# Four chained layers on one core: pools that wait by tile, a reordered norm, the second Sobel layer's first two pairs prepared inside the first's drain, and last pairs in halves

## The chip, the core and the metric

One program runs on one core of a Trainium2 chip. The core has a matrix engine (PE, with its weight loads as PEld), a vector engine (DVE), an activation engine (ACT), a general engine (POOL) and a queue that starts most transfers (SP). They run side by side and wait for each other by semaphores. The metric is the device time of one execution in microseconds (us), as the median of several runs; lower is better.

## The reference, cut to what matters

The input x is an image of 256 rows, 256 columns and 32 channels, in 32-bit floats. Each layer adds to x a function of its group norm (16 groups of two channels over the whole image).

```
x = x + attention(_gn(x))     # softmax over an axis of length 1, so: sigmoid(mn @ Wg) * (mn @ Wv) @ Wo + bo
                              # with mn the layer norm of _gn(x) over the 32 channels
x = x + sobel(_gn(x))         # pooled = 3x3 average; sqrt(grad_x**2 + grad_y**2 + 1e-6), both 3x3 Sobel, per channel
x = x + sobel(_gn(x))
x = x + recurrent(_gn(x))     # two gated cells with a group norm in each, 256 steps along the columns of the image
```

A group norm needs the mean and the variance of the whole image, so no layer can finish its norm before the one ahead has written all of its output.

## The kernel before, in words

**Layout.** The image stays in on-chip memory as `xa` (and `xb`): 128 partitions are four neighbouring columns times 32 channels, the free axis is 64 blocks of four columns by 256 rows. Two blocks are a *pair*, 512 values per partition; all stages work pair by pair, 32 in all (`NST`). Statistics of a pair are taken by `bn_stats` on DVE as soon as the pair is written, and combined by one `bn_aggr`; a matmul with `K_GN` then sums over the partitions of a channel group (first the mean `pm`, then, from `q`, the variance `pv`).

**Input and first norm** (to 35 us). Twenty loads, transposes on PE (L243), copies on ACT (L250), statistics on DVE (L251); `busy_here` puts matmuls on junk behind the first two input groups. Then `bn_aggr` (L267), five `busy_ln` fillers (L272), the mean (L276), the variance (L284), eight records of small bias matmuls (L288), the comparison of the cell's norm weights, and the products of the two weight matrices with the centring (L300). ACT copies the biases (L317) and scales the two products into `wv4` and `wg4` (L319). `shifted(k)` subtracts the mean from a pair, on DVE (L308) but for pair 2 on ACT (L303).

**Layer norm** (35 to 62 us). For each of eight groups of four pairs PE centres (L366), ACT squares (L390), PE averages (L347). After the first group's variance ACT takes the deviation (`std`, L357), DVE the reciprocal `rstds[0]` (L380), and SP issues four broadcast DMAs per pair (`rows`, L328). `scaled(k)` multiplies a pair by its rows: DVE for pair 0, POOL for all others (L338). The deviation of group 0 stands in ACT's order behind the first square of group 2.

**Attention** (58 to 288 us). A list of work with due times, `plan`, is repeated every `step` and sorted; its order is that of the instructions. Matmuls for values and gates (L459), sigmoid on ACT (L468), product on DVE (L472), output matmuls (L485), bias on ACT (L500), residual on POOL (L501), statistics on DVE (L504).

**Sobel layers** (288 to 411 and 411 to 537 us), both by `sobel_layer`. `shift` does the norm's mean and variance, with fillers (`busy`, L580): 3 ahead, 2 between, 16 behind. The mean enters through `m15` and `m75` (L586, L587). Per pair: `convert` (ACT, L601) subtracts 1.5 means; `twos` and `threes` (DVE, L605, L620) sum neighbours along the rows into `pp`, with `ends` (ACT, L610) for the first and last row; `difference` (POOL, L636) makes `dh`; `fours` and `smooth` (L628, L632) make `v` and `sh`, on DVE for pairs 0 and 1 and on POOL for the others. `mixed` (PE, L670) does the step across columns in PSUM, with neighbouring pairs as input. Then `square` (ACT, L676), twice, `total` (DVE, L680), `root` (ACT, L684), `residual` (DVE, L687) and `statistics` (DVE, L690). The second square, the total's second input and the root are one PSUM tile. The order of instructions is again that of a list sorted by due times, one pair each `every` = 3.6; behind the last `mixed` stand seven fillers (L733). The tile pools are opened and closed in each layer.

**Recurrence** (546 to 2490 us): the second layer's output goes to DRAM and back as `xt`, and 256 steps follow.

Of the kernel before, what the change touches and what calls it, by code (L numbers as in the profile page):

```python
# [18 lines left out]
S = 256  # L19
# [4 lines left out]
P = 128  # L24
# [37 lines left out]
def net_kernel(  # L62
# [54 lines left out]
    wv4 = big2.tile([P, D], F32, name="wv4")  # L117
    wg4 = big2.tile([P, D], F32, name="wg4")
# [22 lines left out]
    def new_stats():  # L141
        return small.tile([P, NST, nc.vector.BN_STATS_DIM], F32, name="stats")
# [49 lines left out]
    with tc.tile_pool(name="nat", bufs=6, side="right") as natp, tc.tile_pool(  # L192
# [37 lines left out]
        warm = ps_in.tile([P, P], F32, name="warm", bufs=1)  # L230

        def busy_here(n):
            for _ in range(n):
                nc.tensor.matmul(warm, lhsT=ident, rhs=ident, start=True, stop=True)

        busy_here(7)
        for i, (nat, w0, wl) in enumerate(nats):
            for b2 in range(wl // (2 * J)):
                pt = ps_in.tile([P, 2, 2, P], F32, name="pt")
                for b in range(2):  # L240
                    for h in range(2):
                        lo = (b2 * 2 + b) * J
                        nc.tensor.transpose(  # L243
                            pt[:, b, h, :],
                            nat[:, h, lo : lo + J, :].rearrange("p w c -> p (w c)"),
                            ident,
                        )
                blk = w0 // J + b2 * 2
                dst = xa[:, blk : blk + 2, :].rearrange("p b s -> p (b s)")
                nc.scalar.copy(dst, pt.rearrange("p b h s -> p (b h s)"))  # L250
                nc.vector.bn_stats(stats[:, blk // 2, :], dst)  # L251
            if i < 2:
                busy_here(3)
        table(AF.Sqrt, xa[:, NB - 1, 0:1])

    big3 = second.enter_context(tc.tile_pool(name="big3", bufs=1, side="right"))
# [4 lines left out]
    ps_at = psums.enter_context(tc.tile_pool(name="ps_at", bufs=1, space=PSUM))  # L261
# [12 lines left out]
    busy_ln(5)  # L274
    pm = bank(1)[:, 0:1]
    nc.tensor.matmul(pm, lhsT=kg[:, K_GN, :], rhs=mv[:, 0:1], start=True, stop=True)  # L276
    less = small.tile([P, 1], F32, name="less")
# [7 lines left out]
    pbias = bank(3)  # L285
    for i, w in enumerate(wone):
        for half in range(2):
            nc.tensor.matmul(  # L288
                pbias[:, 2 * i + half : 2 * i + half + 1],
                lhsT=w[:, half * P : (half + 1) * P],  # L290
                rhs=beta,
                start=True,
                stop=True,
            )
    compare()
    psame = bank(6)[0:1, 0:1]
    total_same(psame)
    pws = [bank(4 + i)[:, 0:D] for i in range(2)]
    for pw, w in zip(pws, wgam):
        nc.tensor.matmul(  # L300
            pw, lhsT=cen4.rearrange("c j k -> c (j k)"), rhs=w, start=True, stop=True
        )
    nc.scalar.activation(pair(xb, 2), pair(xa, 2), AF.Identity, bias=less)  # L303
    gstd = small.tile([P, 1], F32, name="gstd")
    nc.scalar.activation(gstd, pv, AF.Sqrt, bias=gn_eps)

    def shifted(k):
        nc.vector.tensor_scalar(pair(xb, k), pair(xa, k), one, less, ALU.mult, ALU.add)  # L308

# [6 lines left out]
    decide(psame, flag)  # L316
    nc.scalar.copy(wbias, pbias[:, 0:4].rearrange("p (i h) -> p i h", i=2))  # L317
    for w, pw in zip((wv4, wg4), pws):
        nc.scalar.activation(w, pw, AF.Copy, scale=scale)  # L319
# [20 lines left out]
    with tc.tile_pool(name="lnq", bufs=9) as lnq:  # L340
# [20 lines left out]
        for g in range(GROUPS):  # L361
# [15 lines left out]
            for j, pc in enumerate(pcs):  # L377
                if g == EARLY + 1 and j == 1:
                    std = deviations()
                    nc.vector.reciprocal(rstds[0], std)  # L380
                    for k in range(3):
                        rowsets[k] = rows_of(k)
                    for k in range(5 * J, NST):
                        shifted(k)
                    for f in reduces:
                        f()
                    for k in range(3):
                        scaled(k)
                sqs.append(lnq.tile([P, 2 * S], F32, name="sq"))
                nc.scalar.activation(sqs[-1], pc, AF.Square)  # L390
# [49 lines left out]
    with tc.tile_pool(name="at", bufs=3) as atp:  # L440
# [13 lines left out]
        def one_of(o, u, j, k):  # L454
            bias = lambda i: wbias[:, i, u : u + 1]
            if o in ("v", "g"):
                rows = slice(j * C, (j + 1) * C)
                w = wv4 if o == "v" else wg4
                nc.tensor.matmul(  # L459
                    take((o, u, j, k)),  # L460
                    lhsT=w[rows, u * P : (u + 1) * P],
# [71 lines left out]
    lw = ctx.enter_context(tc.tile_pool(name="lw", bufs=1))  # L533
# [9 lines left out]
    def sobel_layer(src, dst, moments, before, after, between):  # L543

        stats = new_stats()
        stack = ExitStack()
        kp = stack.enter_context(tc.tile_pool(name="sobk", bufs=1))
        sp = stack.enter_context(tc.tile_pool(name="sob", bufs=2))
        ps_s = stack.enter_context(tc.tile_pool(name="ps_s", bufs=3, space=PSUM))
        ps_c = stack.enter_context(tc.tile_pool(name="ps_c", bufs=2, space=PSUM))  # L550

        along = [kp.tile([P, RING, S], F32, name="sh"), kp.tile([P, RING, S], F32, name="dh")]

        pps = [kp.tile([P, 2, S + 2], F32, name=f"pp{i}") for i in range(2)]
        for pp in pps:
            nc.gpsimd.memset(pp[:, :, 0 : S + 2 : S + 1], 0.0)
        v = {}

        def flat(t):
            return t.rearrange("p b s -> p (b s)")  # L560

        def ring(k):
            b = 2 * k % RING
            return slice(b, b + 2)

        mv = small.tile([P, nc.vector.BN_AGGR_DIM], F32, name="mv")
        m15, m75, std, scale = [
            small.tile([P, 1], F32, name=name) for name in ("m15", "m75", "std", "scale")  # L570
        ]

        def shift():
# [12 lines left out]
            nc.scalar.mul(m15, pm[:, 0:1], -1.5)  # L586
            nc.scalar.mul(m75, pm[:, 0:1], -0.75)  # L587
# [5 lines left out]
            busy(after)  # L593

# [4 lines left out]
        def convert(k):  # L599
            xp = v["xp", k] = ps_c.tile([P, 2, S], F32, name="xp")  # L600
            nc.scalar.activation(flat(xp), pair(src, k), AF.Identity, bias=m15)  # L601

        def twos(k):
            u = v["u", k] = sp.tile([P, 2, S - 1], F32, name="u")
            nc.vector.tensor_add(  # L605
                u, src[:, 2 * k : 2 * k + 2, 0 : S - 1], v["xp", k][:, :, 1:S]
            )

        def ends(k):
            nc.scalar.activation(  # L610
                pps[k % 2][:, :, 1 : S + 1 : S - 1],
                v["u", k][:, :, 0 : S - 1 : S - 2],
                AF.Identity,
                scale=1.5,
                bias=m75,
            )

        def threes(k):
            u, xp = v["u", k], v.pop(("xp", k))
            nc.vector.tensor_add(pps[k % 2][:, :, 2:S], u[:, :, 0 : S - 2], xp[:, :, 2:S])  # L620

        def fill(k):
            return nc.vector if k < 2 else nc.gpsimd

        def fours(k):
            pp = pps[k % 2]
            w = v["v", k] = sp.tile([P, 2, S + 1], F32, name="v")
            fill(k).tensor_add(w, pp[:, :, 0 : S + 1], pp[:, :, 1 : S + 2])  # L628

        def smooth(k):  # L630
            w = v.pop(("v", k))
            fill(k).tensor_add(along[0][:, ring(k), :], w[:, :, 0:S], w[:, :, 1 : S + 1])  # L632

        def difference(k):
            pp = pps[k % 2]
            nc.gpsimd.tensor_sub(along[1][:, ring(k), :], pp[:, :, 0:S], pp[:, :, 2 : S + 2])  # L636
# [34 lines left out]

        def square(k, which):
            pg = flat(v["pg", which, k])
            sq = pg if which else sp.tile([P, 2 * S], F32, name="sq")
            v["sq", which, k] = sq
            nc.scalar.activation(sq, pg, AF.Square, scale=scale)  # L676

        def total(k):
            ss = v["ss", k] = sp.tile([P, 2 * S], F32, name="ss")
            nc.vector.tensor_add(ss, v.pop(("sq", 0, k)), v["sq", 1, k])  # L680

        def root(k):
            mag = v["mag", k] = v.pop(("sq", 1, k))
            nc.scalar.activation(mag, v.pop(("ss", k)), AF.Sqrt, bias=sobel_eps)  # L684

        def residual(k):
            nc.vector.tensor_add(pair(dst, k), pair(src, k), v.pop(("mag", k)))  # L687

        def statistics(k):
            nc.vector.bn_stats(stats[:, k, :], pair(dst, k))  # L690
# [24 lines left out]
        def moved(when, k, part):  # L715
            if k < 2 and part in early:
                return 0.1 * early.index(part) + 0.25 * k
            if k == 1 and part is convert:
                return -0.5
# [4 lines left out]
        todo = [(moved(when, k, part), k, part, args) for when, k, part, args in todo]  # L724
        todo.sort(key=lambda e: e[:2])
        with tc.manual_schedule():
            shift()
            for _, k, part, args in todo:
# [5 lines left out]
                if part is twos and k == 1:  # L734
# [3 lines left out]
        stack.close()  # L738
        return stats

    stats = sobel_layer(xa, xb, stats, 3, 16, [rw.selectors])
    stats = sobel_layer(xb, xa, stats, 3, 16, rw.products())
# [8 lines left out]
    with tc.tile_pool(name="ps_n", bufs=1, space=PSUM) as ps_n:  # L751
# [575 lines left out]
```

## Time and profile before

| what | us |
|---|---|
| three runs | 2498.34, 2499.75, 2502.77 |
| median | 2499.75 |
| profiled execution: its own time | 2498.01 |
| its span, first to last instruction | 2496.2 |
| mean granted clock of PE | 0.992 |
| last statistics of input, layer 0, layer 1, layer 2 end | 30.3, 288.6, 411.4, 537.4 |
| DVE reciprocal of the first deviation starts | 44.0 |
| first Sobel matmul of layers 1 and 2 starts | 298.25, 421.01 |

The span is taken from the trace and is a little shorter than the execution's own time. Profile rows give start, duration, engine, line, operation, output and inputs with their shapes; in square brackets the idle time of that engine before the instruction, and what ended it. An engine that is busy may be busy with fillers.

### The profile page before, as it was taken

The numbers are of one execution on the slowest core, as the hardware profiler recorded it, in microseconds if no ns is written. First come the engines' busy times: TensorE is split into PE (matmuls) and PEld (weight loads), VectorE is DVE, ScalarE is ACT, GpSimd is POOL, SyncE is SP. The second block draws the span as 40 slices with busy tenths as digits, with TensorE's granted clock in tenths as the row PEclk, the third lists the DMA queues.
The fourth block names the chain that finished last, engine by engine and source line by source line (L and its number), as shares of the span: only waits on it lengthen the run. The fifth ranks groups of instructions, "written<-read, shape, count | busy, mean of one in ns | idle before, by whom it ended". The sixth has DMA issues, their size and how long they took to land.

```text
span 2496.2 us, 42484 instructions
## 1 busy us (share of the span) xinstructions
PE 2452.5 (98%) x11615; PEld 1036.2 (42%) x11615; DVE 2242.0 (90%) x6644; ACT 2243.5 (90%) x6876; POOL 1697.2 (68%) x2371
## 2 busy tenths in 40 slices
PE   8999999989999999999999999999999999999997
PEld 4333466653433433333343343333334333333332
DVE  7788898968999999999999999999999999999996
ACT  6788676759999999999999999999999999999997
POOL 1443386847777777777777777777777777777775
PEclk9999999989999999999999999999999999999999
DMA  6887000020101010101010000000000001000000
GB/s 176 50 40 39 2 1 1 1 51 1 22 5 22 5 22 5 22 5 22 7 24 9 19 12 16 13 15 17 10 20 8 21 7 22 5 5 6 5 5 11
DMA packets 117564, 46.78 MB, mean 19 GB/s; under 512 B 77010, under 2 KB 110003, under 8 KB 117316
## 3 DMA queue, kind: packets, MB, share of 16 engines
q1 hardware_dynamic: 115940, 43.80, 12.5%
q8 instruction: 95, 1.56, 0.3%
q14 instruction: 153, 1.25, 0.2%
q10 hardware_dynamic: 1088, 0.13, 0.0%
q0 software_dynamic: 288, 0.03, 0.0%
HBM read 10.37 MB, written 8.39 MB: 8 GB/s over the span
## 4 chain that ended last, share of the span: by engine, by line
PE 71%; DVE 4%; ACT 2%; issue 1%; POOL 0%; DVEq 0%; ACTq 0%; POOLq 0%
PE zz L1137 34%; PE zz L1132 15%; PE zz L1105 9%; PE pt L1197 5%; PE zz L1102 3%; PE pt L1193 2%; PE px L1242 1%; ACT ga L1126 1%; PE px L1232 1%; DVE ve L1150 1%; DVE st L1257 1%; DVE c L1189 1%; DVE c L1181 1%; ACT go L1126 0%; ACT th L1200 0%
## 5 line engine op out<-in xcount | busy, mean ns | idle before, releaser
L1154 POOL TENSOR_TENSOR rs<-ve,mhalf 128x2 f32<-128x2 f32 x1024 | 705.7, 689 | 538.5 <-DVE ve L1150 519.8
L1137 PE MATMUL zz<-wc,hT 128*128 128x512 f32 x2040 | 1059.5, 607 | 0.8 <-DVE hT L1203 0.7
L1126 ACT ACTIVATE ga<-zz,rs 128x128 f32<-128x128 f32 x3072 | 961.9, 370 | 7.7 <-POOL rs L1154 7.4
L1173 POOL TENSOR_TENSOR rs<-ve,mhalf 128x2 f32<-128x2 f32 x1024 | 742.2, 725 | 0.0
L1150 DVE TENSOR_REDUCE ve<-sq 128x4 f32<-128x516 f32 x1024 | 703.6, 687 | 21.5 <-ACT sq L1145 9.5
L1145 ACT ACTIVATE sq<-zz 128x512 f32<-128x512 f32 x1024 | 620.7, 606 | 39.8 <-PE zz L1137 16.7
L1132 PE MATMUL zz<-wc,hT 128*128 128x512 f32 x1024 | 525.0, 594 | 0.0
L1137 PEld LDWEIGHTS zz<-wc,hT 128*128 128x128 f32 x2040 | 317.4, 190 | 337.2 <-DVE c L1189 176.5
L1126 ACT ACTIVATE go<-zz,rs 128x128 f32<-128x128 f32 x1024 | 384.9, 376 | 0.3 <-POOL rs L1173 0.3
L1181 DVE TENSOR_TENSOR c<-ga 128x128 f32<-128x128 f32 x1024 | 295.9, 289 | 87.5 <-ACT ga L1126 56.2
L1185 DVE TENSOR_TENSOR fc<-ga,c 128x128 f32<-128x128 f32 x1020 | 295.6, 290 | 3.2 <-ACT ga L1126 3.2
L1189 DVE TENSOR_TENSOR c<-c,fc 128x128 f32<-128x128 f32 x1020 | 286.3, 281 | 8.8
L1105 PE MATMUL zz<-fx,xt 32*128 32x512 f32 x2048 | 266.6, 589 | 0.0
L472 DVE SCALAR_TENSOR_TENSOR o<-pa,wbias,sg 128x512 f32<-128x512 f32 x256 | 177.4, 744 | 29.8 <-ACT sg L468 20.5
L468 ACT ACTIVATE sg<-pa,wbias 128x512 f32<-128x512 f32 x256 | 160.1, 685 | 45.0 <-PE pa L459 40.3
L1197 PEld LDWEIGHTS pt<-ident,c 128*128 128x128 f32 x512 | 71.1, 139 | 293.3 <-DVE c L1189 284.6
L1200 ACT ACTIVATE th<-pt 128x128 f32<-128x128 f32 x512 | 145.4, 284 | 47.7 <-PE pt L1197 19.1
L1193 PEld LDWEIGHTS pt<-ident,go 128*128 128x128 f32 x512 | 71.1, 139 | 264.6 <-ACT go L1126 256.7
L1209 DVE COPY hT<-pt 128x128 f32<-128x128 f32 x512 | 143.6, 281 | 29.1 <-PE pt L1197 28.8
L1132 PEld LDWEIGHTS zz<-wc,hT 128*128 128x128 f32 x1024 | 160.7, 197 | 11.3 <-issue 9.5
L1200 ACT ACTIVATE th<-c 128x128 f32<-128x128 f32 x512 | 161.8, 316 | 0.8 <-DVE c L1189 0.6
L1203 DVE TENSOR_TENSOR hT<-pt,th 128x128 f32<-128x128 f32 x512 | 145.9, 285 | 16.0 <-ACT th L1200 15.8
(194 smaller groups left out, 3050.6 us busy)
## 6 DMA issues: line engine op xcount, KB each, us to landing
xt<-xa SPq DMA_DIRECT2D x256, 64.0 KB, 2.0
rows<-rstd SPq DMA_DIRECT2D x128, 64.0 KB, 6.4
out_dram<-st SPq DMA_DIRECT2D x252, 32.0 KB, 1.7
nat<-in_x_dram SPq DMA_DIRECT2D x12, 512.0 KB, 9.9
half<-in_x_dram SPq DMA_DIRECT2D x8, 256.0 KB, 7.1
wc<-in_L_conv_W_cell_dram SPq DMA_DIRECT2D x2, 512.0 KB, 5.8
kt<-in_consts_dram SPq DMA_DIRECT2D x1, 640.0 KB, 4.4
kg<-in_consts_dram SPq DMA_DIRECT2D x1, 128.0 KB, 7.0
```

What stands on the lines that cost most here:

```text
L1105: nc.tensor.matmul(v["zz", l, h, t], lhsT=inputs.of(t, r), rhs=fx[r, :], start=False, stop=l == 0 and t == 0,)
L1126: nc.scalar.activation(dst, gates(x, g), func, scale=scale)
L1132: nc.tensor.matmul(get("zz"), lhsT=v["hT", 0, t][:, seqs], rhs=wc[:, l, 0, :], start=False, stop=t == 0)
L1137: nc.tensor.matmul(get("zz"), lhsT=v["hT", l, t - 1][:, seqs], rhs=wc[:, l, 1, :], start=False, stop=True,)
L1145: nc.scalar.activation(sqs[l, h, t % 2][:, :, 0:H], four(get("zz")), AF.Square, scale=float(H**-0.5))
L1150: nc.vector.tensor_reduce(ve, sqs[l, h, t % 2], AX.X, ALU.add)
L1154: nc.gpsimd.tensor_tensor(rs[:, now], get("ve")[:, now], inputs.mhalf[:, now], ALU.pow)
L1173: nc.gpsimd.tensor_tensor(get("rs")[:, 2:4], get("ve")[:, 2:4], inputs.mhalf[:, 2:4], ALU.pow)
L1181: nc.vector.tensor_mul(c, gates(get("ga"), 0), gates(get("ga"), 2))
L1185: nc.vector.tensor_mul(fc, gates(get("ga"), 1), get("c"))
L1189: nc.vector.tensor_add(c, c, get("fc"))
L1200: nc.scalar.activation(th, get("pt")[:, 1, 0:P] if turned else get("c"), AF.Tanh)
```

## The change

Every tile pool opened from the layer norm on gets `reuse_waits="tile"`. As the instructions stand, a user of reused memory then waits for the users of the tile that lay there, rather than for all that the pool has seen; the two Sobel layers share one set of pools and tiles.

In the front, the bias matmuls and their copy move ahead of the norm, with two fillers behind each input group and four at the end; the five fillers ahead of the mean go; the first weight product moves between mean and variance; the shifts of pairs 2, 3 and 4 go to ACT; the two scaled weights become one tile and one instruction; the deviation of group 0 stands ahead of the first square of group 2 instead of behind it.

In the Sobel layers, fillers behind the variance are 9 (layer 1) and 0 (layer 2) instead of 16. While layer 1 drains, convert, twos, ends, threes, difference and fours of layer 2's pairs 0 and 1 are done on its first outputs with **layer 1's** mean. When layer 2's mean is there, `catch_up` corrects: `three` and `twelve` are 3 and -12 times the difference of the means, the first and last column of `v` get `three`, the two edge columns of `dh` get plus or minus `three`, and `smooth` for those pairs becomes one operation that adds `twelve`. The last pair of each layer does square (the first), total, root, residual and statistics in two halves of 256.

```diff
-    busy_ln(5)
+    compare()
     pm = bank(1)[:, 0:1]
     nc.tensor.matmul(pm, lhsT=kg[:, K_GN, :], rhs=mv[:, 0:1], start=True, stop=True)
+    psame = bank(6)[0:1, 0:1]
+    total_same(psame)
+    pws = bank(7)
+    products = [
...
+    products[0]()
     less = small.tile([P, 1], F32, name="less")
...
     nc.tensor.matmul(pv, lhsT=kg[:, K_GN, :], rhs=q, start=True, stop=True)
...
+    products[1]()
+    busy_ln(1)
+
+    def shifted(k):
+        if k in (2, 3, 4):
+            nc.scalar.activation(pair(xb, k), pair(xa, k), AF.Identity, bias=less)
+        else:
+            nc.vector.tensor_scalar(pair(xb, k), pair(xa, k), one, less, ALU.mult, ALU.add)
...
-                if g == EARLY + 1 and j == 1:
+                if g == EARLY + 1 and j == 0:
                     std = deviations()
                     nc.vector.reciprocal(rstds[0], std)
...
-    def sobel_layer(src, dst, moments, before, after, between):
+    sobel = ExitStack()
+    kp = sobel.enter_context(tc.tile_pool(name="sobk", bufs=1, reuse_waits="tile"))
+    sp = sobel.enter_context(tc.tile_pool(name="sob", bufs=2, reuse_waits="tile"))
...
+    AHEAD = 2
...
+    def sobel_layer(rows, dst, moments, before, after, between, following):
+        src = rows.src
+        old = rows.__dict__.get("m15")
+        ahead = AHEAD if old is not None else 0
+        stats = new_stats(NST + 1)
...
+        def catch_up(pm):
+            three, twelve = moves[:, 0:1], moves[:, 1:2]
+            late["twelve"] = twelve
+            nc.scalar.activation(three, pm, AF.Identity, scale=3.0, bias=rows.less3)
+            nc.scalar.activation(twelve, pm, AF.Identity, scale=-12.0, bias=rows.more12)
+            blocks = slice(0, 2 * ahead)
+            for k in range(ahead):
+                w = rows.v["v", k][:, :, 0 : S + 1 : S]
+                nc.scalar.activation(w, w, AF.Identity, bias=three)
+            for column, op in ((0, ALU.add), (S - 1, ALU.subtract)):
+                edge = along[1][:, blocks, column : column + 1]
+                nc.gpsimd.tensor_scalar(edge, edge, three, None, op)
+            rows.centre(pm)
...
+            if ahead:
+                catch_up(pm[:, 0:1])
+            else:
+                rows.centre(pm[:, 0:1])
+                if following:
+                    following.m15, following.m75 = rows.m15, rows.m75
+                    following.less3, following.more12 = moves[:, 2:3], moves[:, 3:4]
+                    nc.scalar.mul(following.less3, pm[:, 0:1], -3.0)
+                    nc.scalar.mul(following.more12, pm[:, 0:1], 12.0)
...
+            if ahead:
+                for k in range(ahead):
+                    w = rows.v.pop(("v", k))
+                    nc.vector.scalar_tensor_tensor(
+                        along[0][:, ring(k), :],
+                        w[:, :, 0:S],
+                        late["twelve"],
+                        w[:, :, 1 : S + 1],
+                        ALU.add,
+                        ALU.add,
+                    )
...
+        def halves(k):
+            return range(2) if k == NST - 1 else (slice(0, 2),)
...
         def total(k):
-            ss = v["ss", k] = sp.tile([P, 2 * S], F32, name="ss")
-            nc.vector.tensor_add(ss, v.pop(("sq", 0, k)), v["sq", 1, k])
+            ss = v["ss", k] = sp.tile([P, 2, S], F32, name="ss")
+            a = v.pop(("sq", 0, k))
+            for b in halves(k):
+                nc.vector.tensor_add(part_of(ss, b), part_of(a, b), part_of(v["sq", 1, k], b))
...
+            if k >= ahead or part not in early + [convert]
+        ]
+        if following:
+            late_in = (NST - 1) * every
+            for k in range(AHEAD):
+                todo += [
+                    (late_in + 2.0 + 4.4 * k, k, following.convert, ()),
+                    (late_in + 3.4 + 4.4 * k, k, following.twos, ()),
+                    (late_in + 5.0 + 4.4 * k, k, following.ends, ()),
+                    (late_in + 5.0 + 4.4 * k, k, following.threes, ()),
+                    (late_in + 9.2 + 3.0 * k, k, following.difference, ()),
+                    (late_in + 9.3 + 3.0 * k, k, following.fours, (nc.gpsimd,)),
+                ]
...
-    stats = sobel_layer(xa, xb, stats, 3, 16, [rw.selectors])
-    stats = sobel_layer(xb, xa, stats, 3, 16, rw.products())
+    first, second_rows = Rows(xa), Rows(xb)
+    stats = sobel_layer(first, xb, stats, 3, 9, [rw.selectors], second_rows)
+    stats = sobel_layer(second_rows, xa, stats, 3, 0, rw.products(), None)
+    sobel.close()
```

## The prediction

> **What bounds the kernel now.** I read the page first (shares and the clock row), then the timeline of the two layer changes, then the waits and timeline of the layer norm, then busy time and clock in single stretches.
>
> ```profile
> PE 2452.5 (98%) x11615; PEld 1036.2 (42%) x11615; DVE 2242.0 (90%) x6644; ACT 2243.5 (90%) x6876; POOL 1697.2 (68%) x2371
> PEclk9999999989999999999999999999999999999999
> ```
>
> PE is busy all the time, but that is an average, and it counts matmuls on junk. The recurrence, about 546 to 2490 us, is untouched; I give it nothing. Time can only move in the first 546 us, where fillers stand at the layer changes:
>
> ```profile
> 405.80 0.69 DVE L680 TENSOR_TENSOR ss<-sq,pg 128x512 f32<-128x512 f32 x1 [0.57 <-ACT sq L676]
> 407.82 0.69 ACT L676 ACTIVATE sq<-pg,scale 128x512 f32<-128x512 f32 x1
> ...
> 410.73 0.69 DVE L690 BATCH_NORM_STATS2 stats<-xb 128x6 f32<-128x512 f32 x1
> 411.46 1.02 DVE L582 BATCH_NORM_AGGREGATE mv<-stats 128x2 f32<-128x192 f32 x1
> ...
> 413.93 7.15 PE L580 MATMUL pg<-kg,ident 128*128 128x256 f32 x32
> ...
> 421.01 1.51 PE L670 MATMUL pg<-dh,kt 128*64 128x256 f32 x11
> ```
>
> Call A the end of layer 1's last statistics, 411.42. The first Sobel matmul of layer 2 (L670) comes at A+9.59: 2.3 us of norm, then 16 fillers (7.15 us; 0.447 each) that cover the preparation of pairs 0 and 1. The third pair starts at 428.22, A+16.80. Layer 1 starts alike, but its third pair needs the POOL row below:
>
> ```profile
> 291.17 7.15 PE L580 MATMUL pg<-kg,ident 128*128 128x256 f32 x32
> 298.25 1.51 PE L670 MATMUL pg<-dh,kt 128*64 128x256 f32 x11
> 301.00 1.04 POOL L632 TENSOR_TENSOR sh<-v 128x512 f32<-128x512 f32 x1
> ```
>
> In the layer norm, a chain reciprocal, broadcast DMAs, scaling decides when attention gets its inputs:
>
> ```profile
> POOL xb L338 <- DMA rows<-rstd: 37.5, 4, 30.7
> DVE rstd L380 <- ACT std L357: 1.7, 1, 1.7
> ```
>
> ```profile
> 42.80 0.60 ACT L390 ACTIVATE sq<-pa 128x512 f32<-128x512 f32 x1 [1.27 <-PE pa L366]
> 43.29 0.68 ACT L357 ACTIVATE std<-pa,ln_eps 128x512 f32<-128x512 f32 x1
> 44.01 3.35 DVE L380 RECIPROCAL rstd<-std 128x512 f32<-128x512 f32 x1 [1.67 <-ACT std L357]
> ```
>
> **The change part by part** (by the profiled execution, 2498.01 us, 1.74 below the median of the three runs, 2499.75).
>
> *Front.* Bias matmuls and fillers go ahead of the norm, one product of the weights ahead of the variance, and the deviation ahead of a square. The mean matmul comes some 0.5 later, because PE first does two fillers per group, the biases and four fillers (4 x 0.28) behind the last inputs; but 1.05 of biases (eight records) and half of the 1.61 of products leave the path to the first layer-norm matmul: 34.8 against 35.46. The deviation now waits for the square of group 1 (ends 41.5), less those 0.6: about 41.05 instead of 43.29. DVE has two shifts of 0.47 fewer, so it is free at 41.7, and the reciprocal starts at 41.8 instead of 44.01. The row DMAs start at its end, POOL's scaling waits for them, and PE's hole of 3.46 us at 60.13 waits for POOL; all shift: **-2.2**. Bounds: -0.5 (only the earlier first matmul is left, another DMA pace swallows the rest) and -4 (the half clock at 40 to 41, in the rows under the rivals, goes too; at most half of 6.8 us, mostly hidden under squares). The pools that wait by tile free the first sigmoid (2.0 us waiting for row DMAs), which is hidden as PE then waits for POOL anyway: 0. What they add is a wait on a finished layer-norm matmul ahead of POOL's scaling, behind which stand the later scalings; finished long before: 0. SP's order is unchanged; the loads of 286.5 lie ahead of their use by 250 us: 0.
>
> *Start of layer 1.* Fillers 16 to 9: 7 x 0.447 = 3.1 off PE. Then data decide: difference 2 on POOL ends 299.92 and smooth 2 at 302.04, so pair 1 ends near 302.5, instead of 305.2: -2.75. Two more small ACT operations stand ahead of the convert (0.07 apart each): +0.15. **-2.6**, bounds -1.5 (POOL's first rows again as slow as 1.36) and -3.1.
>
> *Drain of layer 1.* Inserted, with layer 1's mean: ACT 2 converts (0.68) and 2 ends (0.30); DVE 2 x (0.69+0.67); POOL 2 differences and 2 sums of 1.04. POOL is free (5.63 us idle at 407.85). ACT and DVE have holes of 0.56 to 0.76 on either side of the residual in each of the last pairs, so most fits; what misses its hole delays the chain of squares. Queued behind an inserted sum on DVE is the total of a real pair, for which ACT's root waits. By the order of instructions the total at 405.80 comes at about 406.26 and the last square 407.82 at about 408.3: **+0.45**, bounds 0 (all in holes) and +0.9 (one sum and one convert in full).
>
> *Last pairs in halves.* Chain now 407.82 to 411.42 = 3.60. A half costs ACT 0.47 (the 128x256 weights copy, L319) and DVE about 0.42 (between 0.29 for 128x128, L314, and 0.69 for 128x512). The built program's waits let only the first square and the total overlap: the first half root waits for the second half total, the first half residual for the second half root, since square, total's input and root share one PSUM tile. So 0.47 + 2x0.42 + 2x0.47 + 2x0.42 + 2x0.42 + four handovers of 0.05 = 4.13: **+0.55** per layer, two layers **+1.1**. Bounds: -0.7 (everything overlaps: five halves, one more, handovers = 2.9) and +0.7. The Trainium skill (PSUM — Partial Sum Buffer, section "PSUM bank collisions raise a hardware error") says that accesses of two engines to one bank and quadrant must be kept apart by bank, not by address; it speaks against this part, and no run here shows a collision. By the rule the term is +0.55 per layer as taken; without it, -0.7.
>
> *Start of layer 2.* Gone after the mean: DVE's u, pp, v, sh of two pairs (4.1 to 5.5 us), 2 differences, 2 converts, 2 ends, 16 fillers. Added after it: ACT three and twelve (0.17 each) and two edge operations, POOL two edges, DVE sh(0), sh(1) in one step each (0.75, the scalar_tensor_tensor row of 0.744). From A: aggregate ends 1.06, mean matmul 1.12 to 1.53, three 1.56, edges on ACT to 2.35, m75 2.54, d and q to 2.98, variance matmul 3.4, sh(0) 3.0 to 3.77, sh(1) 4.47. The POOL edge has no row; between 0.19 (COPY 128x4) and 0.45 (a 128x128 TENSOR_SCALAR); nearest is 0.19, two of them ready by 2.7, ahead of PE. First Sobel matmul at A+3.45, pair 0 ends 6.2, pair 1 needs smooth 2 on POOL (8.14 to 9.18) and ends 9.7, pair 2 starts A+9.9 against A+16.80: **-6.9**. Bounds -7.2 (PE gap-free) and -4 (POOL and DVE collide as at 416.95, where 1.04 and 0.69 became 1.36 and 1.41, and pairs 2 to 4 wait). Nothing covers PE there any more: a late sh(3) or sh(4) (some 16.2 against a need at 16.35) is paid in full.
>
> Sum: -2.2 - 2.6 + 0.45 + 1.1 - 6.9 = **-10.15**, 2487.9 for the profiled execution; by the median 2489.6.
>
> **The rivals.**
>
> *More is won* (chance 0.10). Halves overlap (-0.7 for +0.55, twice: -2.5) or the layer norm loses its half clock (to -4): -13 to -15. For it: the fillers between input groups; against: the waits in the order.
>
> *Less is won* (0.14). The start-ups meet their upper bounds: -0.5 - 1.5 + 0.9 + 1.4 - 4 = -3.7, more likely -6: 2494.
>
> *The clock falls* (0.11). Stretches of the trace; the third number from the right is the granted clock, after it DMA share and GB/s:
>
> ```profile
> 33.00:34.00 1.00, 1.00 (x11) 0.95 (x10) 1.00 (x3) 0.28 (x2) 0.00 (x0) 1.00 0.15 57
> 40.00:41.00 1.00, 1.00 (x12) 0.20 (x8) 1.00 (x4) 1.00 (x4) 0.00 (x0) 0.50 0.00 0
> 60.00:61.00 1.00, 0.13 (x1) 0.00 (x0) 1.00 (x1) 0.54 (x2) 0.00 (x0) 1.00 0.78 29
> 62.00:64.00 2.00, 0.41 (x2) 0.42 (x4) 0.33 (x1) 1.26 (x2) 1.26 (x1) 0.50 0.93 28
> 286.00:288.00 2.00, 0.35 (x4) 0.01 (x1) 1.43 (x3) 0.00 (x0) 1.12 (x6) 1.00 0.06 16
> ```
>
> Read: after one hole of 3.46 us the clock was 0.50 until 68.55; holes of 1.2 us (42.84) and 1.68 (286.35) did nothing. The fillers now go from both Sobel starts, leaving short N=1 matmuls and holes under 1 us. Should that count as idle, 6.8 us at half clock cost up to 3.4 per start: -10.15 + 3.4 = -6.75, with both -3.35 (2496.4). [...]
>
> *Slower* (0.05). The Sobel pace becomes DVE's or POOL's: PE now runs ahead with no stock of prepared pairs, and DVE's five operations of 0.69 in a pair equal PE's 3.43. One mechanism, DVE slowed by POOL beside it as at 417.45. At +0.16 us a pair over 64 pairs the gain is gone; above +0.24 it is slower by over 0.2%. At +0.3: +9, 2509. Against: when DVE lagged in layer 1 (totals at 306.79, 310.14, 313.50) it ran 3.354 a pair and caught up.
>
> *It doesn't do what it says*: if the drain work delays layer 1 by as much as it saves (four ACT, four DVE operations in full, 1.96 + 2.72 = 4.7), the whole is -5.9; it is within "less".
>
> **How the numbers follow.** The sum as worked out has 0.60, with its own range of 2486.5 to 2493; the others as named. The likeliest is 2489.6. The range takes in "more" up to -15.5 (2484.3) at the low end and "less" and one fallen clock at the high end, up to the sum of the bounds, -3.7 (2496). About 0.2% (5 us) is what a measurement of this kernel can tell: faster means below 2494.75. Faster: 0.60 + 0.10 + about two thirds of "less" and of "the clock" (0.16) = 0.86; same 0.09; slower 0.05.
>
> **What would show it.** In the changed profile: the first reciprocal of the layer norm near 41.8 and PE's hole near 58 to 61.4; the clock row at both Sobel starts at 1.00; layer 2's first mixed matmul 3.4 to 3.6 us behind layer 1's last statistics and its third pair 9.9 behind; the last pair's chain 4.1 long, with roots after both totals; the last square of layer 1 0.4 to 0.5 late. Wrong would be: PE waiting for POOL's smooth of pairs 2 to 5, a clock of 0.50 beyond 286 us ahead of 540, or totals spaced over 3.5 in mid-layer.

## The result and the profile after

The changed kernel takes 2490.59 us (median of six runs, 2488.91 to 2492.59) against 2499.74 us for the one before (2498.34 to 2502.77): a ratio of 0.996, 95% interval 0.9949 to 0.997, or 9.15 us less. The profiled execution took 2489.37 us with a span of 2487.0, which is 9.2 less than the span before. The prediction was 2489.6, that is 10.15 less.

The two traces can be compared stage by stage, because in the Sobel layers the milestones of kernels with the same stage repeat from trace to trace within some 0.05 us (pair 1 of layer 2 lies 10.46 to 10.49 behind the aggregate in all eleven kernels with the preparation). The front and the recurrence do not repeat like that, as the experiments show. "Aggregate" below is the start of the `bn_aggr` of a layer's norm; "pair 1" is the first square of the second pair (`sq`).

| stage | before, us | after, us | moved | predicted |
|---|---|---|---|---|
| start to the first reciprocal of the layer norm | 44.01 | 41.84 | -2.17 | -2.2 |
| from there to layer 1's aggregate | 244.63 | 244.50 | -0.13 | 0 |
| layer 1: aggregate to pair 1 | 16.74 | 14.56 | -2.18 | -2.6 |
| layer 1: pair 1 to the last square | 102.44 | 102.60 | +0.16 | +0.45 |
| layer 1: last square to layer 2's aggregate | 3.64 | 3.83 | +0.19 | +0.55 |
| layer 2: aggregate to pair 1 | 16.69 | 10.49 | -6.20 | -6.9 |
| layer 2: pair 1 to the last square | 105.71 | 105.71 | 0.00 | 0 |
| layer 2: last square to the last aggregate | 3.62 | 3.80 | +0.18 | +0.55 |
| last aggregate to the first recurrent matmul | 9.04 | 10.48 | +1.44 | 0 |
| the rest | 1949.68 | 1949.19 | -0.49 | 0 |
| sum | 2496.2 | 2487.0 | -9.20 | -10.15 |

The change of layers, in the timeline of the changed kernel (start, duration, engine, line, operation; `x2` is two halves shown as one row):

```profile
403.50 0.84 ACT L748 ACTIVATE sq<-pg,scale 128x256 f32<-128x256 f32 x2 [0.19 <-PE pg L734]
404.09 0.74 DVE L754 TENSOR_TENSOR ss<-sq,pg 128x256 f32<-128x256 f32 x2
404.86 0.99 ACT L760 ACTIVATE pg<-ss,sobel_eps 128x256 f32<-128x256 f32 x2 [0.53 <-DVE ss L754]
405.88 0.75 DVE L766 TENSOR_TENSOR xb<-xa,pg 128x256 f32<-128x256 f32 x2 [1.05 <-ACT pg L760]
...
407.33 1.05 DVE L655 BATCH_NORM_AGGREGATE mv<-stats 128x2 f32<-128x198 f32 x1
...
410.69 1.51 PE L734 MATMUL pg<-dh,kt 128*64 128x256 f32 x11
...
417.89 1.94 PE L734 MATMUL pg<-dh,kt 128*64 128x512 f32 x8
```

The first Sobel matmul of layer 2 starts 3.36 us behind the aggregate, where it was 9.55. In the last pair the roots start when both totals are done (404.09 + 0.74 = 404.83) and the residuals when both roots are done: only square and total overlap, as read from the waits. At the start of layer 1 PE now waits where it had fillers:

```profile
293.00 1.51 PE L734 MATMUL pg<-dh,kt 128*64 128x256 f32 x11
...
297.67 0.13 PEld L734 LDWEIGHTS pg<-dh,kt 128*64 128x64 f32 x1 [1.03 <-POOL dh L617]
...
299.78 0.13 PEld L734 LDWEIGHTS pg<-sh,kt 128*64 128x64 f32 x1 [1.06 <-POOL sh L613]
```

In the layer norm the deviation is early (it follows the squares on ACT without a gap), and the reciprocal stands behind DVE's shifts, a group of 15 that ends at 41.92:

```profile
34.99 6.93 DVE L314 TENSOR_SCALAR xb<-xa,one,less 128x512 f32<-128x512 f32 x15
...
40.22 0.77 ACT L365 ACTIVATE std<-pa,ln_eps 128x512 f32<-128x512 f32 x1
...
41.84 3.35 DVE L388 RECIPROCAL rstd<-std 128x512 f32<-128x512 f32 x1
```

Ahead of the recurrence the granted clock (third number from the right in the last fence, a stretch of 1 us) is already 0.50. Before (first fence), it fell only at 546.42, when the six records of px, the matmuls right ahead of the first recurrent one (`zz`), were nearly done, 1.55 us in all; now (second fence) it falls at 534.43 and they take 2.90.

```profile
545.03 1.55 PE L1225 MATMUL px<-xa,ident 128*128 128x256 f32 x6 [1.59 <-DVE cst L961]
```

```profile
534.98 2.90 PE L1322 MATMUL px<-xa,ident 128*128 128x256 f32 x6 [1.59 <-DVE cst L1058]
```

```profile
535.00:536.00 1.00, 1.00 (x3) 0.82 (x4) 0.10 (x1) 0.00 (x0) 0.00 (x0) 0.50 0.55 128
```

### The profile page after: what moved, and what is told of

It reads as the page before. It is cut to its first block, busy times and chain, and to the rows that moved or that the text cites. A ratio compares the mean times of both kernels' runs of the same rounds, so it can differ in the third digit from the quotient of the medians.

```text
span 2487.0 us, 42458 instructions
## 1 busy us (share of the span) xinstructions
PE 2445.1 (98%) x11597; PEld 1031.7 (41%) x11597; DVE 2238.9 (90%) x6646; ACT 2245.9 (90%) x6888; POOL 1698.7 (68%) x2373
## 4 chain that ended last, share of the span: by engine, by line
PE 71%; DVE 4%; ACT 2%; issue 1%; POOL 0%; DVEq 0%; ACTq 0%; POOLq 0%
PE zz L1234 34%; PE zz L1229 16%; PE zz L1202 9%; PE pt L1294 5%; PE zz L1199 3%; PE pt L1290 2%; PE px L1339 1%; ACT ga L1223 1%; PE px L1329 1%; DVE ve L1247 1%; DVE st L1354 1%; DVE c L1286 1%; DVE c L1278 1%; ACT go L1223 0%; ACT th L1297 0%
## 5 line engine op out<-in xcount | busy, mean ns | idle before, releaser
L466 PE MATMUL pa<-xb,wvg 32*128 32x512 f32 x1024 | 164.9, 642 | 4.0 <-POOL xb L346 3.7
```

## The experiments

Each kernel is the changed one with one edit, or with the few that the text names. Its median stands beside that of the kernel before in the same series (2501.38, 2502.42 and 2501.24). The expected times start from 2490.59, which was measured beside 2499.74, so a kernel's ratio says more than its time; the ratios carry some 3 us of uncertainty, and stages are read from the traces, one per kernel.

**Layer 2's start: preparation or fillers?** Without the preparation, fillers 16 again:

```diff
-    stats = sobel_layer(first, xb, stats, 3, 9, [rw.selectors], second_rows)
-    stats = sobel_layer(second_rows, xa, stats, 3, 0, rw.products(), None)
+    stats = sobel_layer(first, xb, stats, 3, 9, [rw.selectors], None)
+    stats = sobel_layer(second_rows, xa, stats, 3, 16, rw.products(), None)
```

> The changed kernel without the preparation of layer 2's first two pairs in layer 1's drain, and with the 16 fillers behind layer 2's variance again (the front, layer 1's 9 fillers and the halves stay). Call A the end of layer 1's last statistics. Theory (the way from A to the first mixed matmul is what the preparation shortens, nothing else): first mixed matmul at A+9.6 instead of A+3.39, first square of pair 1 at A+16.7 instead of A+10.5, the rest of layer 2 shifted by 6.2, the last square of layer 1 0.17 earlier as its drain holds nothing extra: about 2496.6 us. Rival (the drain work costs layer 1 nearly what it saves layer 2): under 2493.

Measured: 2499.57 against 2501.38 (ratio 0.9991, 0.9982 to 1.0001), 3 us over the expected 2496.6; in its trace the recurrence, from the last aggregate on, took 4.18 us longer than in the changed kernel, with the same instructions. First mixed matmul 9.65 behind the aggregate, pair 1 at 16.78: 6.29 later than in the changed kernel, as expected. From layer 1's pair 1 to layer 2's aggregate it takes 106.43 with the preparation and the same without: the drain work costs layer 1 nothing, and the +0.16 of the table is not its doing. My expectation had put that 0.17 down to it; where it comes from is not shown.

The same with 9 fillers (the edit against the kernel just above):

```diff
-    stats = sobel_layer(second_rows, xa, stats, 3, 16, rw.products(), None)
+    stats = sobel_layer(second_rows, xa, stats, 3, 9, rw.products(), None)
```

> As before it, but with 9 fillers behind layer 2's variance, so that only fillers are taken off. Theory (with fewer fillers the preparation itself is in the way, as it was in layer 1, where the square of pair 1 moved by 2.2 and not by the 3.1 of the fillers): first mixed matmul at A+6.7, square of pair 1 at A+14.5, 2494.4 us. Rival (only the fillers were in the way): square of pair 1 at A+13.6, 2493.5 us.

Measured: 2496.90 against 2501.38 (0.9982, 0.9973 to 0.9992). First mixed matmul at 6.62, pair 1 at 14.62, so theory: three microseconds of fillers less gave 2.2. The trace of this kernel shows the rest as PE's waits for POOL:

```profile
413.08 4.13 PE L653 MATMUL pg<-kg,ident 128*128 128x256 f32 x18
...
417.14 1.51 PE L734 MATMUL pg<-dh,kt 128*64 128x256 f32 x11
...
421.91 0.13 PEld L734 LDWEIGHTS pg<-dh,kt 128*64 128x64 f32 x1 [1.13 <-POOL dh L617]
...
424.03 0.19 PEld L734 LDWEIGHTS pg<-sh,kt 128*64 128x64 f32 x2 [1.06 <-POOL sh L613]
```

So of layer 2's 6.2 us some 2.2 can be had by taking fillers off; the other 4.1 needs the preparation moved.

**Layer 1's fillers.**

```diff
-    stats = sobel_layer(first, xb, stats, 3, 9, [rw.selectors], second_rows)
+    stats = sobel_layer(first, xb, stats, 3, 16, [rw.selectors], second_rows)
```

> The changed kernel with 16 fillers in layer 1 again instead of 9. Theory: layer 1's squares all 2.2 later against the end of layer 0's last statistics (pair 1: 16.8 behind it instead of 14.6), 2492.8 us. Rival (the seven fillers are worth their own 3.1): 17.7 behind, 2493.7. Rival (they cover the clock and cost nothing): no shift, 2490.6.

Measured: 2494.67 against 2501.38 (0.9974, 0.9964 to 0.9985). Pair 1 is 16.82 behind the aggregate instead of 14.56: 2.26, the theory's 2.2 and not 3.1 or 0. In no trace of this study did the granted clock fall between 80 and 531 us, so it fell at no Sobel start, whatever the fillers there (16, 9 or none).

**The last pairs.** First whole again:

```diff
-        stats = new_stats(NST + 1)
+        stats = new_stats()
...
-            return range(2) if k == NST - 1 else (slice(0, 2),)
+            return (slice(0, 2),)
```

> The changed kernel with the last pairs whole again. Theory (the halves run one behind the other, but half operations follow each other without the gap between whole ones): the way from the last square to the end of the last statistics 3.60 instead of 3.80 in layer 1, 3.6 instead of 3.76 in layer 2, together -0.35, 2490.2 us, which only the trace can show. The prediction's term: -1.1, 2489.5. Rival (the halves pay): +1 and more.

Measured: 2493.14 against 2501.38 (0.9968, 0.9955 to 0.998). Last square to aggregate 3.61 in both layers, against 3.83 and 3.80: the halves as they stand cost 0.41 in all. That is their sign as predicted and 0.4 of their size. Then with the root in a tile of its own:

```diff
-            mag = v["mag", k] = v.pop(("sq", 1, k))
+            mag = v.pop(("sq", 1, k))
+            if k == NST - 1:
+                mag = sp.tile([P, 2, S], F32, name="mag", bufs=1)
+            v["mag", k] = mag
```

> The changed kernel with the root of the last pair written to a tile of its own in on-chip memory, not over the second square in PSUM; then a half root waits for its own half total, a half residual for its own half root. Theory (the shared tile is what kept the halves apart): from the last square to the end of the last statistics 3.1 instead of 3.80 in layer 1 and 3.76 in layer 2, together -1.35, 2489.2 us. Rival (the halves are bound by their own operations and handovers): 3.6 or more.

Measured: 2491.53 against 2501.24 (0.9963, 0.995 to 0.9977). Last square to aggregate 3.10 and 3.03, together 1.50 less than in the changed kernel, as the theory had it. Its timeline:

```profile
402.27 0.84 ACT L748 ACTIVATE sq<-pg,scale 128x256 f32<-128x256 f32 x2 [0.19 <-PE pg L734]
402.87 0.73 DVE L754 TENSOR_TENSOR ss<-sq,pg 128x256 f32<-128x256 f32 x2
403.31 0.91 ACT L763 ACTIVATE mag<-ss,sobel_eps 128x256 f32<-128x256 f32 x2 [0.20 <-DVE ss L754]
403.85 0.82 DVE L769 TENSOR_TENSOR xb<-xa,mag 128x256 f32<-128x256 f32 x2 [0.24 <-ACT mag L763]
```

The roots start 0.44 behind the totals, not 0.77: the shared PSUM tile was what kept the halves apart. Whether the waits go by the tile or by the bank that it lies in, no run here tells apart. The Trainium skill (PSUM — Partial Sum Buffer, section "PSUM bank collisions raise a hardware error") asks for waits by bank; the 0.77, a first half root that starts only behind the second half total, agrees with it. No run here shows a collision.

**The front.** The place of the deviation:

```diff
-                if g == EARLY + 1 and j == 0:
+                if g == EARLY + 1 and j == 1:
```

> The changed kernel with the deviation of group 0 behind the first square of group 2 again, as in the kernel before. Theory (in the changed kernel the reciprocal waits for DVE's shifts, which end at 41.84, not for the deviation, which ends at 40.99): the deviation 0.6 later, the reciprocal at 41.8 to 41.9, no change of the time. Rival (the reordering is what brings the front's 2.2): reciprocal at 43.5 to 44.0, everything behind it 1.7 to 2.2 later.

Measured: one run, 2492.03. The first aggregate itself moves from trace to trace (30.06 to 32.02, with the landing of the inputs), so I read from it. The reciprocal is 10.74 behind the first aggregate, in the changed kernel 10.69: theory, although the raw 42.76 is neither. With the deviation 1.0 later the reciprocal now follows it at once:

```profile
42.05 0.68 ACT L365 ACTIVATE std<-pa,ln_eps 128x512 f32<-128x512 f32 x1
...
42.76 3.35 DVE L388 RECIPROCAL rstd<-std 128x512 f32<-128x512 f32 x1
```

The fillers of the input stage, and both:

```diff
-            busy_here(2)
-        biases()
-        busy_here(4)
+            if i < 2:
+                busy_here(3)
+        biases()
```

> The changed kernel with the fillers of the input stage as in the kernel before (three behind each of the first two groups only), the deviation still ahead of the square. Theory: the granted clock is again 0.50 for some 6.8 us from about 34, groups 0 to 2 of the layer norm slow down, the deviation starts at 40.5 to 41.2, the reciprocal at 41.8 to 42.0 behind the shifts: at most 0.2 later. Rival (the clock is what brings the front's 2.2): reciprocal at 43 to 44.

> Both undone, fillers and place of the deviation. Theory (either alone is enough, as DVE's shifts stand behind both): the deviation at 42.8 to 43.3 behind a square that waits for a half-speed matmul, the reciprocal 1.5 to 2.2 later than in the changed kernel, and with it the end of layer 0. Rival (neither matters, the gain is the two shifts taken from DVE): reciprocal at 41.8 to 42.0.

Measured: one run each, 2492.73 and 2496.03. Reciprocal 12.50 and 13.27 behind the aggregate (before: 13.66). So my theory fell for both. With the clock at 0.50 for 10.2 and 6.8 us from 31 and 32, it is the deviation itself that is late, and DVE waits for it:

```profile
43.38 0.74 ACT L365 ACTIVATE std<-pa,ln_eps 128x512 f32<-128x512 f32 x1
...
44.16 3.35 DVE L388 RECIPROCAL rstd<-std 128x512 f32<-128x512 f32 x1 [1.37 <-ACT std L365]
```

The reciprocal goes with the clock, then. But fillers alone do not decide the clock: other kernels here have the changed kernel's fillers and order, and fell or did not.

| us at 0.50 near 34 | reciprocal behind the first aggregate, us (deviation ahead of the square) |
|---|---|
| 0 (changed kernel, fill16_first) | 10.69, 10.68 |
| 3.4 (root_sbuf, warm_rec, whole_pairs) | 10.69, 10.73, 11.26 |
| 6.8 (no_prep_9) | 11.94 |
| 10.2 (no_prep_16, pools_default) | 12.13, 12.39 |

With 6.8 us of fall the late deviation gave 13.27 and 13.66, the early one 11.94: its place may be worth 1.3 to 1.7 then, which is not shown, as those two kernels also lack the new fillers and one of them is the kernel before. Without a fall it is worth nothing (std_late). The mean fall with the new fillers (nine traces with otherwise the changed front, std_late included) is 4.2 us, without them (three traces) 8.0: that they help is likely, not shown.

Last, the shifts that hold the reciprocal when the clock is high:

```diff
-                for k in range(J, 5 * J):
+                for k in range(J + 1, 4 * J):
...
-                    for k in range(5 * J, NST):
+                    for k in range(4 * J, NST):
```

> The changed kernel with the shifts of pairs 16 to 19 behind the first reciprocal on DVE instead of ahead of it, and the second, needless shift of pair 4 on ACT left out. Theory (DVE's shifts hold the reciprocal): reciprocal at 40.2 to 40.4 instead of 41.84, row DMAs, POOL's scaling and the end of layer 0 1.4 to 1.6 earlier, 2489.1 us. Rival (the row DMAs have a pace or a start of their own): reciprocal earlier, end of layer 0 less than 0.5 earlier.

Measured: 2494.58 against 2501.24 (0.9973, 0.9964 to 0.9983). That interval overlaps the changed kernel's 0.9949 to 0.997, so it is not shown to be slower, but a gain of 1.5 is not there. The reciprocal gained 0.38 (10.31 behind the aggregate), since the deviation became the wait; the layer norm ended later (second deviation 16.8 behind the first, 15.45 in the changed kernel), as centring now waits for shifts behind the reciprocal.

```profile
41.10 3.35 DVE L388 RECIPROCAL rstd<-std 128x512 f32<-128x512 f32 x1 [1.37 <-ACT std L365]
...
44.96 2.41 PE L374 MATMUL pa<-xb,cen 32*32 32x512 f32 x32 [0.53 <-DVE xb L314]
```

Then the clock was 0.50 for 13.7 us from 62, not 6.8, and POOL's first scaling to the aggregate took 228.37 instead of 226.10. Other kernels show the same long fall (warm_rec 13.7 and 227.79), so whether this edit causes it stays open. The time goes with it over the 14 traces: from the reciprocal to layer 1's aggregate they took 244.29 to 244.63 where the fall near 60 lasted 6.8 us (nine traces), and 245.81 to 246.79 where it lasted 10.2 to 17.1 (five).

**The pools.**

```diff
-    big3 = second.enter_context(tc.tile_pool(name="big3", bufs=1, side="right", reuse_waits="tile"))
+    big3 = second.enter_context(tc.tile_pool(name="big3", bufs=1, side="right"))
...
```

and so at every other pool. The two Sobel layers still share one set of pools.

> The changed kernel with all pools waiting in the default manner. Theory (the waits by tile free only instructions that were not on the path): no change within 0.3 us in any stage, 2490.6 us; the first sigmoid waits for row DMAs again, while PE waits for POOL anyway. Rival (the waits by tile carry part of the gain): layer 0's end or layer 2's first mixed matmul 0.5 us or more later.

Measured: 2492.18 against 2502.42 (0.9965, 0.9952 to 0.9978). The first sigmoid waits 2.0 us for row DMAs again, as before; from the reciprocal to the last aggregate the stages are within 0.15 of the changed kernel (first scaling 18.37 behind it, 18.40; pair 1 of layer 1 14.61, of layer 2 10.49). The pools move nothing that counts.

**The recurrence's start.** Three fillers behind the last small matmuls (`pk`):

```diff
+        junk = psum.tile([P, S], F32, name="junk", tag="junk", bufs=1)
+        for _ in range(3):
+            nc.tensor.matmul(
+                junk, lhsT=self.ident, rhs=self.wc[:, 0, 0, 0:S], start=True, stop=True
+            )
```

> The changed kernel with three fillers of 256 columns behind the last small matmuls ahead of the recurrence. Theory (PE's pause of 1.6 us there, after low use, lets the granted clock fall to 0.50 at 534.3, and the first matmuls of the recurrence, 2.90 instead of 1.55 us, pay for it): no fall at 534, the first recurrent matmul 1.35 earlier against the end of the norm, 2489.2 us. Rival (the clock falls by a beat of its own, or because of what lies ahead): the fall stays, or comes a few us later and takes as much.

Measured: 2489.87 against 2501.24 (0.9954, 0.9939 to 0.9969). The fall at 534 is gone, px takes 1.53, and the first recurrent matmul is 9.18 behind the last aggregate instead of 10.48: 1.30 of the 1.35.

```profile
534.65 1.54 PE L1059 MATMUL junk<-wc,ident 128*128 128x256 f32 x6
...
536.45 1.53 PE L1327 MATMUL px<-xa,ident 128*128 128x256 f32 x6 [0.26 <-DVE cst L1063]
```

A fall of 10.2 us follows at 543, within the first recurrent steps; the changed kernel had 13.7 there, from 541. The twelve traces without these fillers have the fall begin 7.0 to 8.9 behind the last aggregate, the two with them 14.6 and 12.3. At DVE's first transposition of results (`st`) warm_rec is 105.84 behind the last aggregate, the changed kernel 107.09. But no_prep_9, without these fillers, is 105.39, and also had only 10.2 us at half clock: that the fillers delay the fall is shown, that they shorten it is not.

All three edits together:

> The three together: root in a tile of its own, reciprocal ahead of the last shifts, fillers ahead of the recurrence. Theory: the gains add, -1.35 -1.5 -1.35 = -4.2, 2486.4 us. Rival (the clock's falls move when the stages move, and give part of it back): between 2487.5 and 2490.

Measured: 2490.09 against 2501.24 (0.9959, 0.9945 to 0.9972). In its trace the last pairs (3.11 and 3.03) and the recurrence's start (9.18) keep their gains, 2.8 in all; the front gives some back (first scaling to aggregate 227.40, 10.2 us of fall). Its ratio and warm_rec's lie within the interval of the changed kernel's 0.996: neither is shown to be faster.

## Why the prediction was right, and where it was not

- **The whole.** 2490.59 lies 1.0 from the forecast, 9.15 saved of 10.15. In the traces the last aggregate comes 10.15 earlier (537.48 and 527.33), which is the forecast to the hundredth, but by luck: two gains were 1.1 too large together and two losses 1.0. The recurrence then gives 0.95 back.
- **Start of layer 2, -6.9, was -6.20.** Mechanism right, size off. The first mixed matmul came at 3.36 as forecast (3.45 behind A). The step "pair 1 ends 9.7" failed: PE needs 7.2 from the first mixed matmul to pair 2 in both kernels (410.69 to 417.89 now), and the row was there (421.01 to 428.22). The gain is the 9.55 - 3.36 between the first matmuls. PE's cover was not needed: the later pairs kept their spacing to 0.02.
- **Start of layer 1, -2.6, was -2.18.** The wait that takes the fillers' place was named (POOL's smooth 2); it ends 13.39 behind the aggregate now, as the rows had it (302.04 - 288.64 = 13.40). But PE has 1.1 us of pair 1's matmuls behind it (299.73 to 300.86), where the prediction allowed 0.46.
- **Drain, +0.45, was 0 for the work put in.** POOL, ACT and DVE took all of it in their holes: 106.43 with and without. The delay read from the order of instructions did not reach the chain.
- **Halves, +1.1, were +0.41 against whole pairs.** The waits were read rightly. The size failed at the term of 0.42 and 0.47 for every half: two halves behind each other took 0.74 on DVE, and 0.84 and 0.99 on ACT. The rival "halves overlap" needed another tile; then it gave 1.5.
- **Front, -2.2, was -2.17 by the milestone, but not by the step given.** The aggregate came 0.80 later, the reciprocal 2.97 earlier against it. The deviation does wait for the square of group 1, as said, but that was taken to end at 41.5 less 0.6; the deviation started at 40.22, as the clock had not fallen. That DVE's shifts end at 41.7 was nearly right and hid the error. And the -2.17 is that of a trace without a fall: with the same front the reciprocal came up to 1.7 later behind the aggregate (12.39 for 10.69), so that it met the forecast is luck in part.
- **The clock.** The rival put its fall at the Sobel starts. It did not fall there, and the holes of up to 1.7 us had not made it fall before. It fell ahead of the recurrence, at 534.43, which is the sign named under "Wrong would be" (0.50 beyond 286 us ahead of 540), at another place than meant. I had given the recurrence "nothing"; its first matmul came 1.44 later. But the kernel before had as much half clock there, 17.1 us in all, only from 546.42 on, and at DVE's first transposition of results (`st`) 0.37 of the 1.44 is left (107.09 behind the last aggregate, 106.72 before). The rest of the 0.95 came later, in instructions that are the same, and its cause is open.
- **The hole of 3.46 us.** The prediction read the half clock near 62 us as coming after this hole. The trace of the kernel before has PE idle from 60.13 to 63.59 and the clock at 0.50 from 61.73 on, 1.60 us into the hole (the row below, whose mean clock is 0.86); and at 34.42 it fell though matmuls filled 2.63 of the 3.41 us ahead. The length of a hole alone did not decide it.

```profile
61.00:62.00 1.00, 0.00 (x0) 0.00 (x0) 1.00 (x1) 0.00 (x0) 0.00 (x0) 0.86 1.11 64
```

- **The slower side** (Sobel pace set by DVE or POOL) did not come: pair 1 to the last square of layer 2 is 105.71 in both.

## What to carry to other kernels

Fillers over a wait are a sign that something could be done there; taking them off gave 2.2 of 3.1 us, and moving the hidden work into the drain of the layer before gave the other 4.1, at no cost to the drain. A split into halves pays only if each half's output lies where the next half's readers are not: look at the waits of the built program, and move the output to a tile of its own. When an edit moves a stage, check where the next quiet stretch of PE falls and count its clock, but count it from a mark behind the whole stretch: a fall that only comes earlier can delay the first matmul by 1.4 us and what follows by a quarter of that.

## What was not expected of the hardware

The stretches at half clock came in lengths of 3.4, 6.8, 10.2, 13.7, 17.1 and 20.5 us, those aside that the end of the program cuts short, and in the same instructions they came or not: 0 to 10.2 us near 34, 6.8 to 17.1 near 60, 10.2 to 20.5 in all near the recurrence's start. In the changed kernel's trace the clock fell at 534.43 although PE had been busy for 1.00, 1.00, 1.00 and 0.39 of the four microseconds from 530 on (with matmuls of one column and on 33 rows among them). No trace has a fall behind 3.41 us without a matmul: ahead of the 44 falls between 25 and 2400 us, matmuls filled 0.42 to 3.31 of the last 3.41 us. The Trainium skill (TensorE: Matmul & The Clock Gate, Part 1) describes a free-running window of about 3.4 us; the lengths agree with that. Its threshold of one idle window, read as a window without a matmul, covers none of these 44 falls, and the measurement decides; what counts as idle is open here.

The recurrence, whose steps are the same instructions in all these kernels, ran at one of two paces for nearly a whole execution: eight steps took 60.02 to 60.03 us in some traces and 60.08 to 60.09 in others (about 1.8 us over the whole recurrence). One trace per kernel cannot tell whether that goes with the execution or with the kernel. With the clock's falls it makes several us that belong to no edit, which is why stages were read from the traces.
